# A four-layer graph stack on one core: gate rows transposed on VectorE, layer 3 aggregated in four column tiles, a plan that counts tiling changes

## Chip, core and metric

The kernel runs on one core of a Trainium2 chip. The core has five engines that work side by side, each through its own instructions in order: TensorE (matmul; PE in the profile, its weight loads PEld), VectorE (DVE), ScalarE (ACT), GpSimd (POOL) and SyncE (SP, which here only issues DMAs). The metric is the device time of one launch in microseconds, lower is better. All data is f32 unless said otherwise.

## What is computed

32 graphs of 512 nodes with 256 features share one adjacency matrix with self loops. Each graph passes through four attention layers; after each comes a residual sum and a layer norm. Cut to the layers' cores:

```python
# layer 0: 8 heads of 32, with its own residual, norm and a two-matmul block behind it
scores = einsum('fnhd,fmhd->fhnm', q, k) / sqrt(D);  scores = where(adj > 0, scores, -1e9)
t = einsum('fhnm,fmhd->fnhd', softmax(scores), v);   x = layernorm(x + t) ...
# layer 1: one head, additive scores
h = x @ W;  e = leaky_relu(s1[:, :, None] + s2[:, None, :], 0.2);  e = e + (1 - mask) * -1e9
out = softmax(e) @ h
# layer 2: one head, product scores
e = leaky_relu((x @ W1) @ (x @ W2).T, 0.2);  e = where(adj > 0, e, -1e12)
out = relu(softmax(e) @ (x @ W3))
# layer 3: 4 heads of 64, additive scores
e = e_src[:, :, None, :] + e_dst[:, None, :, :];  e = where(e >= 0, e, 0.2 * e), masked
out = elu(softmax(e) @ q)
```

## The kernel before

The launch runs `fast_path` (L630), which computes everything and a flag; `general_path` follows only if the flag says that values were out of bounds, and does not run with these inputs.

**A plan made in the host program.** `fast_path` does not issue instructions as it goes. Each small group of instructions on one engine is entered in a `Plan` (L459) with its engine, an assumed time in ns, what it reads and writes, and a function that issues it. `place` (L522) then simulates the engines and picks, again and again, the group that can start first; among those of one engine that can start at the same time, the one with the earliest due time. When a group is picked, its buffers are assigned and its instructions issued, so the plan fixes the order of every engine's instructions and nothing else. The assumed times never reach the chip. The due time of a group (L1364) is `PACE` times the graph's number plus an offset that is interpolated from eleven numbers (`TENTHS`; others for the first four and the last five graphs). Up to six graphs (`WAYS`) are under way at once; they share 8 PSUM banks, 8 tiles `p` for attention weights and the other buffers at L677. DMAs in flight are a sixth "engine" in the plan.

**Tilings of TensorE.** Matmuls use the array in four ways, which the plan numbers: 0 the full array (projections, aggregation of layers 1 and 2, transposes); 1 four row tiles of 32 (`exps`, L1027: scores of four heads of layer 0 at once); 2 four column tiles of 32 (aggregation of layer 0, L1093, and the row sums with the constant `pick`, L1065 and L1281); 3 two column tiles of 64 (aggregation of layer 3, L1306). The plan adds `SWITCH` (100 ns) to TensorE's time when the tiling changes. `STAY`, which could put off a change, is 0. An f32 matmul shows as two instructions in the profile.

**Gates of layers 1 and 3** (`gates`, L1167). Their scores are sums of a source and a target term, so the weights are products of exponentials. For the source side the kernel needs exp(0.8 s) of all 512 nodes as a row, on every partition. ScalarE computes it with nodes on partitions into `gs` (L1179, 4 or 16 columns), TensorE transposes `gs` (L1182), ScalarE copies the result from PSUM to `gT` (L1184), SyncE stores `gT` to a DRAM buffer `row` (L1186) in one DMA and loads it back, repeated over all partitions, into `G` (L1192). VectorE then builds the weights from `G` (L1211, L1290) and masks them (L1214, L1297).

**Row sums** of the softmax come for layers 0 and 3 from tiles `p` that DMAs add up (issued by GpSimd, L972) and a few matmuls with `pick`; in the last graph, by matmuls alone. SyncE also issues a copy for them (L1112), the loads of x (L1347) and the stores of the output (L1354).

Of the kernel before, what the change touches and what calls it, by code (L numbers as in the profile page):

```python
# [17 lines left out]
P = 128  # L18
# [12 lines left out]
PACE = 81.87  # L31
STAY = 0.00
START = (0, 10.17, 59.24, 97.18, 85.64)
EARLY = 186.52

TENTHS = (0, 35.72, 65.32, 68.92, 152.58, 202.32, 246.27, 266.73, 356.34, 362.66, 490.49)
FIRST = (
    (0, 35.72, 65.32, 62.35, 138.44, 202.98, 246.27, 266.73, 356.34, 362.66, 490.49),
    (-28.44, 35.72, 73.98, 55.02, 197, 202.32, 246.27, 266.73, 356.34, 362.66, 490.49),
    (-31.13, 30.72, 65.32, 68.92, 152.58, 202.32, 246.27, 266.73, 356.34, 362.66, 490.49),  # L40
    (0, 35.77, 65.37, 68.97, 152.63, 202.32, 246.27, 266.73, 356.34, 362.66, 490.49),)
LAST = (
    (0, 35.72, 65.32, 68.92, 152.58, 202.32, 246.27, 266.73, 354.73, 363.36, 490.49),
    (0, 35.72, 65.32, 68.92, 152.58, 202.32, 246.27, 266.73, 356.34, 362.66, 490.49),
    (0, 35.72, 65.32, 68.92, 152.58, 202.26, 246.21, 266.73, 356.34, 412.91, 557.81),
    (-0.21, 35.51, 65.11, 68.71, 152.37, 202.11, 226.96, 232.14, 316.44, 341.17, 500.04),
    (-6.23, 29.49, 59.09, 8.93, 61.49, 76.67, 155.18, 191.54, 257.43, 316.36, 394.47),)
# [391 lines left out]
SIGNAL = 70  # L439
SWITCH = 100  # L440
# [11 lines left out]
class Op:  # L452
    def __init__(self, engine, ns, run, graph, rank, port, lag, tiling):
        self.engine, self.ns, self.run, self.graph, self.rank = engine, ns, run, graph, rank
        self.port, self.lag, self.tiling = port, lag, tiling
        self.then, self.missing, self.slots, self.ready = [], 0, [], 0.0


class Plan:  # L459
# [19 lines left out]
    def __call__(self, engine, ns, run, reads=(), writes=(), port=False, lag=0, tiling=0):  # L479
        op = Op(engine, ns, run, self.graph, self.rank, port, lag, tiling)  # L480
# [41 lines left out]
    def place(self, urgency, ways, stay=0.0, early=1e12, run=True):  # L522
# [13 lines left out]
        port, port_by, end, tiling = 0.0, None, 0.0, 0  # L536
        self.trace = []
# [21 lines left out]
        while todo:  # L559
            choice = None  # L560
            for e, ops in waiting.items():
                found = []
                for op in ops:
# [8 lines left out]
                    if choice and t > choice[0]:  # L572
                        continue
                    wants = {}
                    for s in op.slots:
                        if s.index is None:
                            wants.setdefault(s.kind, []).append(s)
                    if all(safe(op, kind, new) for kind, new in wants.items()):
                        for kind, new in wants.items():
                            t = max(t, sorted(free[kind])[len(new) - 1][0])  # L580
                        if op.tiling != tiling and e is PE:
                            due += stay
                        found.append((t, due, op))
                if found:
                    best = min(found, key=lambda f: f[:2])
                    if choice is None or best[0] < choice[0]:
                        choice = best
            assert choice, "no instruction can be placed: too few buffers"
            t, _, op = choice
            if op.engine is PE and op.tiling != tiling:  # L590
                t, tiling = max(t, engines[PE] + SWITCH), op.tiling
            waiting[op.engine].remove(op)
# [6 lines left out]
            engines[op.engine] = t + op.ns  # L599
            if op.port:  # L600
                port, port_by = t + op.ns, op.engine
            done = t + op.ns + op.lag + SIGNAL
# [7 lines left out]
            for other in op.then:  # L610
                other.missing -= 1
                other.ready = max(other.ready, done if other.engine != op.engine or op.lag
                                  else t + op.ns)
                if not other.missing:
                    waiting[other.engine].append(other)
# [4 lines left out]
            ended[op.graph] = max(ended.get(op.graph, 0.0), t + op.ns + SIGNAL)  # L620
# [9 lines left out]
def fast_path(  # L630
# [50 lines left out]
        "e1": (6, [P, NC * H3]), "gs": (2, [P, NC * H3]), "ri": (3, [P, NC * H0]),  # L681
        "gT": (2, [NC * H3, P]),
# [27 lines left out]
    nc.vector.memset(far, 0.0)  # L710

# [36 lines left out]
    def prepare():  # L748
# [30 lines left out]
        for c in range(NC):  # L779
            dve(690, lambda c=c: nc.vector.tensor_scalar(  # L780
                T(edges)[:, c, :], T(raws[c // 2])[:, c % 2, :].bitcast(I32), 0.0, None, ALU.is_gt),
                [(raws[c // 2], c)], [(edges, c)])
        for m in range(NC):
# [6 lines left out]
            plan(PE, 440, run, [edges], [bank])  # L790
            dve(690, lambda bank=bank, m=m: nc.vector.tensor_copy(T(edge_t)[:, m, :], T(bank)),
                [bank], [(edge_t, m)])
            dve(400, lambda m=m: nc.vector.tensor_scalar(
# [23 lines left out]
        for c in range(NC):  # L817
            off = Slot("e")
            dve(690, lambda c=c, off=off: nc.vector.tensor_tensor(
                T(off), T(edges)[:, c, :], T(raws[c // 2])[:, c % 2, :].bitcast(I32), ALU.not_equal),  # L820
                [edges, (raws[c // 2], c)], [off])
            dve(690, lambda c=c, off=off: nc.vector.tensor_reduce(
# [65 lines left out]
    def evac(dst, to, src, frm, n, writes):  # L888

        act(170 + n * 0.84, lambda: nc.scalar.activation(to(T(dst)), frm(T(src)), AF.Copy),  # L890
            [src], writes)

    def transposed(src, width=0):

        dst = Slot("t")
        for c0 in range(0, NC, 2):
# [7 lines left out]
            plan(PE, 440, run, [(src, c0), (src, c0 + 1)], [bank])  # L904
# [4 lines left out]
    def project_t(w, col, xT, dst, k):  # L909
# [7 lines left out]
        plan(PE, 1720, run, [w, xT], [bank])  # L917
        evac(dst, lambda t: t[:, k, :], bank, lambda b: b, N, [(dst, k)])

    def project(xT, w, col, width, dst):  # L920

        per = N // width
        for c0 in range(0, NC, per):
# [9 lines left out]
            plan(PE, per * KC * width * 1.69, run, [w, xT], [bank])  # L933
# [4 lines left out]
    def normalise(y, dst):  # L938

        st, mv, rs, nm = Slot("st"), Slot("mv"), Slot("rs"), Slot("rs")  # L940
        for c in range(NC):
# [3 lines left out]
            dve(600, run, [(y, c)], [(st, c), (mv, c)])  # L945
# [3 lines left out]
        act(420, deviations, [mv], [rs])  # L949
        dve(300, lambda: nc.vector.scalar_tensor_tensor(  # L950
            T(nm), T(mv)[:, :, 0], -1.0, T(rs), ALU.mult, ALU.mult), [mv, rs], [nm], True)
        for c in range(NC):
            act(600, lambda c=c: nc.scalar.activation(  # L953
# [3 lines left out]
    def add(dst, a, b, c0, row=None, op=ALU.add):  # L957

        w = slice(c0, c0 + 2)
        pool(1500 if row is None else 1850, lambda: nc.gpsimd.tensor_tensor(  # L960
# [17 lines left out]
    def sums_back(sm):  # L978
# [8 lines left out]
        plan(PE, 440, run, [sT], [bank])  # L987
# [19 lines left out]
    def heads_out(oT, rinv, heads):  # L1007
# [3 lines left out]
        for c0 in range(0, NC, 2):  # L1011
# [7 lines left out]
            plan(PE, 440, run, [oT, rinv], [bank])  # L1019
            dve(680, lambda bank=bank, c0=c0: nc.vector.tensor_tensor(  # L1020
# [6 lines left out]
    def exps(kT, qT, g, m, p):  # L1027
# [8 lines left out]
        plan(PE, 970, run, [(kT, g), (qT, g)], banks, tiling=1)  # L1036
        for j in range(J):
            act(600, lambda j=j: nc.scalar.activation(  # L1038
# [14 lines left out]
    def layer0(xs, at_once):  # L1053
# [14 lines left out]
        def collect(g, m, ps):  # L1068

            if at_once:  # L1070
                for c in (m - 1, m):
                    plan(PE, 870, lambda c=c: sums(g, ps[c], g == 0 and c == 0,
# [8 lines left out]
        for g in range(KC):  # L1081
            av, ps = Slot("bank"), []
            for m in range(NC):
                p = Slot("p")
                exps(kT, qT, g, m, p)
                dve(2420, lambda p=p, m=m: nc.vector.tensor_tensor(  # L1086
# [9 lines left out]
                plan(PE, 880, run, [(v, m), p], [av], tiling=2)  # L1096
# [9 lines left out]
        else:  # L1106
# [7 lines left out]
            plan(PE, 870, lambda: sums(2, low, True, True), [low], [sm], tiling=2)  # L1114
# [3 lines left out]
        dve(370, lambda: within(T(rinv)[:, :NC * H0], R_MIN, R_MAX), [rinv], [], True)  # L1118
# [12 lines left out]
        for d in range(KC):  # L1131
# [6 lines left out]
            plan(PE, 1720, run, [w1_sb, nT], [bank])  # L1138
            act(690, lambda bank=bank, d=d: nc.scalar.activation(
                T(hT)[:, d, :], T(bank), AF.Relu, bias=T(b1_sb)[:, d:d + 1]), [bank, b1_sb], [(hT, d)])  # L1140
        f = Slot("y")
        for c0 in range(0, NC, 2):
# [9 lines left out]
            dve(680, lambda bank=bank, c0=c0: nc.vector.tensor_tensor(  # L1152
# [4 lines left out]
        for c0 in range(0, NC, 2):  # L1157
            w, parts = slice(c0, c0 + 2), (c0, c0 + 1)
            dve(690, lambda w=w: nc.vector.tensor_tensor(
                T(f)[:, w, :], T(f)[:, w, :], T(g2_row).unsqueeze(1).to_broadcast([P, 2, C]),  # L1160
                ALU.mult), [(f, c) for c in parts] + [g2_row], [(f, c) for c in parts], True)
            dve(690, lambda w=w: nc.vector.tensor_tensor(
# [4 lines left out]
    def gates(v, heads, G):  # L1167
# [5 lines left out]
        def check():  # L1173
# [4 lines left out]
        gs, bank, gT, row = Slot("gs"), Slot("bank"), Slot("gT"), Slot("row")  # L1178
# [3 lines left out]
        plan(PE, 150, lambda: nc.tensor.transpose(T(bank)[:R, :P], T(gs)[:, :R], ident),  # L1182
             [gs], [bank])
# [253 lines left out]
```

## Time and profile before

| what | value |
|---|---|
| median of 3 runs | 2895.84 us (2895.43 to 2897.85) |
| profiled execution: span, first to last instruction | 2891.7 us |
| mean granted TensorE clock | 0.993 |
| L1182 gate transposes on TensorE | 64, mean 272 to 276 ns each, pipelined |
| L1184 copies of them on ScalarE | 64, mean 252 to 253 ns |
| L1186 stores of the gate rows | 64 DMAs of 2 or 8 KB, issue 317 ns (median) |
| L1306 aggregation of layer 3 | 1024 instructions, 242.8 us busy |
| L1093 aggregation of layer 0 | 2048 instructions, 275.2 us busy |
| L1034 scores of layer 0 | 2048 instructions, 302.6 us busy |
| wait of VectorE for a gate row, L1211 | 27.6 us in 21 times |

The span is that of one profiled execution. The time outside a launch's span cannot be seen in it; the median of the runs lies 4.1 us above the span. A matmul's mean duration includes the pipeline behind it: the next one starts earlier than it ends, so rates are read from one start to the next. In the groups, the numbers after the bar are busy us, mean ns of one, idle us of the engine before them and what ended it.

### The profile page before, as it was taken

The numbers are of one execution on the slowest core, as the hardware profiler recorded it, in microseconds if no ns is written. First come the engines' busy times: TensorE is split into PE (matmuls) and PEld (weight loads), VectorE is DVE, ScalarE is ACT, GpSimd is POOL, SyncE is SP. The second block draws the span as 40 slices with busy tenths as digits, with TensorE's granted clock in tenths as the row PEclk, the third lists the DMA queues.
The fourth block names the chain that finished last, engine by engine and source line by source line (L and its number), as shares of the span: only waits on it lengthen the run. The fifth ranks groups of instructions, "written<-read, shape, count | busy, mean of one in ns | idle before, by whom it ended". The sixth has DMA issues, their size and how long they took to land.

```text
span 2891.7 us, 39629 instructions
## 1 busy us (share of the span) xinstructions
PE 2832.4 (98%) x14014; PEld 1579.2 (55%) x14014; DVE 2443.2 (84%) x4076; ACT 1885.5 (65%) x4104; POOL 865.9 (30%) x962
## 2 busy tenths in 40 slices
PE   8899999999999999999999999999999999999996
PEld 3355555555555555555555555555555555554562
DVE  5568888888888988888988888988888888888877
ACT  4566667666667666666666666666676666676553
POOL 1233333232333232332232333232333323333312
PEclk9999999999999999999999999999999999999998
DMA  6856777777777777777777777776776777775125
GB/s 168 169 110 142 150 159 164 154 144 160 145 161 153 159 149 158 149 160 157 147 152 150 157 157 155 152 160 144 162 157 150 155 153 146 161 163 115 35 55 132
DMA packets 101149, 424.44 MB, mean 147 GB/s; under 512 B 10256, under 2 KB 46224, under 8 KB 59152
## 3 DMA queue, kind: packets, MB, share of 16 engines
q0 software_dynamic: 49600, 325.08, 57.2%
q1 hardware_dynamic: 51344, 96.75, 11.6%
q8 instruction: 113, 1.85, 0.2%
q14 instruction: 92, 0.75, 0.1%
HBM read 63.38 MB, written 17.10 MB: 28 GB/s over the span
## 4 chain that ended last, share of the span: by engine, by line
PE 92%; DVE 3%; DMA 2%; issue 1%; ACT 1%; POOL 0%; SPq 0%; ACTq 0%; DVEq 0%; POOLq 0%
PE bank L929 15%; PE bank L915 11%; PE bank L1034 9%; PE bank L1093 8%; PE bank L1306 8%; PE bank L1221 7%; PE bank L1244 7%; PE bank L1260 7%; PE bank L902 5%; PE bank L1136 4%; PE bank L1148 4%; PE bank L1017 2%; DMA p<-p 1%; PE bank L1281 1%; PE bank L1065 1%
## 5 line engine op out<-in xcount | busy, mean ns | idle before, releaser
L972 POOL DMA_DIRECT2D p<-p x372 | 322.3, 871 | 1787.8 <-DMA p<-p 568.4
L1086 DVE TENSOR_TENSOR p<-p,edge_t 128x2048 f32<-128x2048 f32 x256 | 618.2, 2424 | 59.7 <-ACT p L1038 59.5
L890 ACT ACTIVATE t<-bank 128x512 f32<-128x512 f32 x640 | 373.5, 596 | 384.2 <-PE bank L915 125.4
L1038 ACT ACTIVATE p<-bank 128x512 f32<-128x512 f32 x1024 | 537.9, 599 | 89.2 <-PE bank L1034 87.6
L943 DVE BATCH_NORM_STATS2 st<-y 128x6 f32<-128x256 f32 x768 | 315.9, 411 | 35.6 <-POOL y L960 26.0
L1290 DVE TENSOR_SCALAR p<-p,e,e 128x512 f32<-128x512 f32 x512 | 331.3, 680 | 1.0 <-DMA p<-row 1.0
L960 POOL TENSOR_TENSOR y<-y,x 128x512 f32<-128x512 f32 x192 | 273.7, 1432 | 158.2 <-ACT y L1265 100.1
L1297 DVE TENSOR_TENSOR p<-p,edge_t 128x2048 f32<-128x2048 f32 x128 | 304.9, 2382 | 2.2
L1034 PE MATMUL bank<-t,t 32*128 32x512 f32 x2048 | 302.6, 644 | 0.0
L953 ACT ACTIVATE x<-y,rs,rs 128x256 f32<-128x256 f32 x512 | 277.6, 596 | 24.6 <-DVE rs L950 24.3
L1093 PE MATMUL bank<-p,v 128*32 128x512 f32 x2048 | 275.2, 609 | 12.5 <-DVE p L1086 9.7
L1306 PE MATMUL bank<-p,v 128*64 128x512 f32 x1024 | 242.8, 605 | 3.6 <-DVE p L1297 3.6
L915 PE MATMUL bank<-t,wqkv 128*128 128x512 f32 x512 | 241.6, 595 | 0.7 <-ACT t L890 0.7
L1221 PE MATMUL bank<-v,p 128*128 128x257 f32 x1024 | 237.8, 381 | 0.7 <-DVE p L1214 0.4
L890 ACT ACTIVATE v<-bank 128x264 f32<-128x264 f32 (+2 forms) x384 | 176.5, 460 | 90.2 <-PE bank L929 88.3
L1260 PE MATMUL bank<-v,p 128*128 128x257 f32 x1024 | 227.4, 380 | 0.0
L1244 PE MATMUL bank<-t,t 128*128 128x512 f32 x512 | 225.1, 592 | 0.0
L1221 PEld LDWEIGHTS bank<-v,p 128*128 128x128 f32 x1024 | 189.5, 190 | 40.3 <-issue 16.3
L1260 PEld LDWEIGHTS bank<-v,p 128*128 128x128 f32 x1024 | 194.2, 190 | 28.6 <-issue 1.3
L1034 PEld LDWEIGHTS bank<-t,t 32*128 32x128 f32 x2048 | 86.0, 184 | 169.5 <-issue 101.5
L944 DVE BATCH_NORM_AGGREGATE mv<-st 128x2 f32<-128x6 f32 x768 | 139.7, 182 | 26.3
L902 PE MATMUL bank<-ident,x 128*128 128x128 f32 x1024 | 148.9, 279 | 11.7 <-DMA x<-in_x_dram 7.7
(121 smaller groups left out, 4148.8 us busy)
## 6 DMA issues: line engine op xcount, KB each, us to landing
p<-p POOLq DMA_DIRECT2D x248, 1024.0 KB, 7.2
p<-p POOLq DMA_DIRECT2D x124, 512.0 KB, 5.7
p<-row SPq DMA_DIRECT2D x32, 1024.0 KB
x<-in_x_dram SPq DMA_DIRECT2D x32, 512.0 KB
out_dram<-x SPq DMA_DIRECT2D x32, 512.0 KB
p<-p SPq DMA_DIRECT2D x31, 512.0 KB
e<-row SPq DMA_DIRECT2D x32, 256.0 KB
t<-in_adj_dram SPq DMA_DIRECT2D x4, 256.0 KB
```

The source lines that it names most:

```text
L890: act(170 + n * 0.84, lambda: nc.scalar.activation(to(T(dst)), frm(T(src)), AF.Copy), [src], writes)
L915: nc.tensor.matmul(T(bank), T(w)[:, i, col:col + P], T(xT)[:, i, :], start=(i == 0), stop=(i == KC - 1))
L929: nc.tensor.matmul(T(bank)[:, j * width:(j + 1) * width], T(xT)[:, k, (c0 + j) * P:(c0 + j + 1) * P], T(w)[:, k, col:col + width], start=( ...
L1034: nc.tensor.matmul(T(banks[j]), T(kT)[r, g, m * P:(m + 1) * P], T(qT)[r, g, :], start=True, stop=True)
L1038: act(600, lambda j=j: nc.scalar.activation(T(p)[:, j, :], T(banks[j]), AF.Exp, scale=1.0 / math.sqrt(D0)), [banks[j]], [(p, j)])
L1086: dve(2420, lambda p=p, m=m: nc.vector.tensor_tensor(T(p), T(p), T(edge_t)[:, m, :].unsqueeze(1).to_broadcast([P, J, N]), ALU.mult), [p, ( ...
L1093: nc.tensor.matmul(T(av)[j * D0:(j + 1) * D0, :], T(v)[:, m, h * D0:(h + 1) * D0], T(p)[:, j, :], start=(m == 0), stop=(m == NC - 1))
L1221: nc.tensor.matmul(T(bank)[:, :C + 1], T(p)[:, m, c * P:(c + 1) * P], T(v)[:, m, 2:C + 3], start=(m == 0), stop=(m == NC - 1))
L1244: nc.tensor.matmul(T(bank), T(xT)[:, k, m * P:(m + 1) * P], T(qT)[:, k, :], start=(k == 0), stop=(k == KC - 1))
L1260: nc.tensor.matmul(T(bank)[:, :C + 1], T(p)[:, m, c * P:(c + 1) * P], T(v)[:, m, :C + 1], start=(m == 0), stop=(m == NC - 1))
L1290: nc.vector.tensor_scalar(T(p)[:, 2 * m + i, :], T(G)[:, h, :], T(e1)[:, r:r + 1], T(e02)[:, r:r + 1], ALU.mult, ALU.max)
L1306: nc.tensor.matmul(T(av)[i * D3:(i + 1) * D3, :], T(q)[:, m0 + m, 2 * H3 + h * D3:2 * H3 + (h + 1) * D3], T(p)[:, 2 * m + i, :], start=(m0 ...
```

## The change

1. `gates`: the transpose of `gs` on TensorE and ScalarE's copy are replaced by one transpose on VectorE, which turns 32x32 blocks. `gs` and `gT` become 128x32 tiles; `gs` is cleared once at the start by GpSimd. Since each block of 32 nodes ends up on its own 32 partitions, the store becomes four DMAs, with 32 values to a row.
2. Layer 3's aggregation uses four column tiles of 32 (tiling 2) in place of two of 64 (tiling 3). Twice as many matmuls of half the width compute the same thing.
3. The plan's order. When it picks a group for TensorE, the key is now the due time, plus an entry from `CHANGE` by the tilings left and entered, plus `LATE` times the wait of TensorE, in which a change counts at least `SWITCH` plus an entry time. Due times have an offset for each of a graph's 339 groups (`DUE`), with additions for the first four and last five graphs. The assumed times of nearly all groups are new numbers, each group has an additional `tail` until others see its result, and `START`, `PACE` and `EARLY` are new.

The row sums are computed as before. Of part 3 the diff shows the rules and some of the many new assumed times:

```diff
-PACE = 81.87
-STAY = 0.00
-START = (0, 10.17, 59.24, 97.18, 85.64)
-EARLY = 186.52
-TENTHS = (0, 35.72, 65.32, 68.92, 152.58, 202.32, 246.27, 266.73, 356.34, 362.66, 490.49)
+PACE = 82.89
+EARLY = 237.58
+LATE = 58.47
+CHANGE = ((0, -15.02, -0.86), (-10.53, 0, -9.19), (16.15, -1.96, 0))
+START = (13.01, 7.41, 43.1, 109.34, 103.14)
+DUE = (
...
-SIGNAL = 70
-SWITCH = 100
+SIGNAL = 40
+SWITCH = 92
+ENTRY = {1: 121, 2: 34}
+TAIL = {PE: 160, DVE: 85, ACT: 120, POOL: 45, SP: 0, DMA: 0}
...
-    def __call__(self, engine, ns, run, reads=(), writes=(), port=False, lag=0, tiling=0):
-        op = Op(engine, ns, run, self.graph, self.rank, port, lag, tiling)
+    def __call__(self, engine, ns, run, reads=(), writes=(), port=False, lag=0, tiling=0, entry=104):
+        op = Op(engine, ns, run, self.graph, self.rank, port, lag, tiling, ENTRY.get(tiling, entry))
...
-                    if choice and t > choice[0]:
+                    if e is not PE and choice and t > choice[0]:
                         continue
...
+                    key = t, due
+                    if e is PE:
+                        wait = t - engines[PE]
+                        if op.tiling != tiling:
+                            wait = max(wait, SWITCH) + op.entry
+                        key = due + change[tiling][op.tiling] + late * wait, 0
+                    if best and key >= best[0]:
+                        continue
                     if all(safe(op, kind, new) for kind, new in wants.items()):
-                        for kind, new in wants.items():
-                            t = max(t, sorted(free[kind])[len(new) - 1][0])
-                        if op.tiling != tiling and e is PE:
-                            due += stay
-                        found.append((t, due, op))
...
-            done = t + op.ns + op.lag + SIGNAL
+            done = t + ns + op.lag + op.tail + SIGNAL
...
-        "e1": (6, [P, NC * H3]), "gs": (2, [P, NC * H3]), "ri": (3, [P, NC * H0]),
-        "gT": (2, [NC * H3, P]),
+        "e1": (6, [P, NC * H3]), "gs": (2, [P, 32]), "ri": (3, [P, NC * H0]),
+        "gT": (2, [P, 32]),
...
+    for gs in buffers["gs"]:
+        nc.gpsimd.memset(gs, 0.0)
...
-        plan(PE, 970, run, [(kT, g), (qT, g)], banks, tiling=1)
+        plan(PE, 858, run, [(kT, g), (qT, g)], banks, tiling=1)
         for j in range(J):
-            act(600, lambda j=j: nc.scalar.activation(
+            act(482, lambda j=j: nc.scalar.activation(
...
-        gs, bank, gT, row = Slot("gs"), Slot("bank"), Slot("gT"), Slot("row")
+        gs, gT, row = Slot("gs"), Slot("gT"), Slot("row")
...
-        plan(PE, 150, lambda: nc.tensor.transpose(T(bank)[:R, :P], T(gs)[:, :R], ident),
-             [gs], [bank])
-        act(270, lambda: nc.scalar.activation(T(gT)[:R, :], T(bank)[:R, :P], AF.Copy),
-            [bank], [gT])
-        plan(SP, 450, lambda: nc.sync.dma_start(T(row)[:R, :], T(gT)[:R, :]), [gT], [row], lag=2000)
+        dve(70, lambda: nc.vector.transpose(T(gT), T(gs)), [gs], [gT])
+
+        def store():
+            with nc.allow_non_contiguous_dma(reason="32 values a row"):
+                for j in range(0, P, 32):
+                    nc.sync.dma_start(T(row)[:R, j:j + 32], T(gT)[j:j + R, :])
+        plan(SP, 600, store, [gT], [row], lag=2000)
...
-                            h = 2 * k + i
-                            nc.tensor.matmul(T(av)[i * D3:(i + 1) * D3, :],
-                                             T(q)[:, m0 + m, 2 * H3 + h * D3:2 * H3 + (h + 1) * D3],
-                                             T(p)[:, 2 * m + i, :], start=(m0 + m == 0),
-                                             stop=(m0 + m == NC - 1))
-                plan(PE, 1770, run, [q, p], [av], tiling=3)
+                            for w in range(i * D3, (i + 1) * D3, 32):
+                                nc.tensor.matmul(T(av)[w:w + 32, :],
+                                                 T(q)[:, m0 + m, 2 * H3 + k * P + w:2 * H3 + k * P + w + 32],
+                                                 T(p)[:, 2 * m + i, :], start=(m0 + m == 0),
+                                                 stop=(m0 + m == NC - 1))
+                plan(PE, 1742, run, [q, p], [av], tiling=2)
...
     def due(b, rank):
-        times = FIRST[b] if b < len(FIRST) else LAST[b - B] if b >= B - len(LAST) else TENTHS
-        tenth = min(int(when[rank]), 9)
-        return PACE * b + times[tenth] + (times[tenth + 1] - times[tenth]) * (when[rank] - tenth)
+        late = FIRST[b] if b < len(FIRST) else LAST[b - B] if b >= B - len(LAST) else None
+        time = PACE * b + DUE[rank]
+        if late:
+            tenth = min(int(when[rank]), 9)
+            time += late[tenth] + (late[tenth + 1] - late[tenth]) * (when[rank] - tenth)
+        return time
...
-        plan.place(urgency, WAYS, 1e3 * STAY, 1e3 * EARLY)
+        plan.place(urgency, WAYS, 1e3 * EARLY, LATE, [[1e3 * c for c in row] for row in CHANGE])
```

## The prediction

> **What bounds it now.** I read the page first, for its busy shares, its clock row and its chain.
>
> ```profile
> span 2891.7 us, 39629 instructions
> ...
> PE 2832.4 (98%) x14014; PEld 1579.2 (55%) x14014; DVE 2443.2 (84%) x4076; ACT 1885.5 (65%) x4104; POOL 865.9 (30%) x962
> ...
> PEclk9999999999999999999999999999999999999998
> ...
> PE 92%; DVE 3%; DMA 2%; issue 1%; ACT 1%; POOL 0%; SPq 0%; ACTq 0%; DVEq 0%; POOLq 0%
> ```
>
> TensorE is busy for 98% of the span and makes up 92% of the chain that ended last. Next come the waits of TensorE, longest first, and the busy times between 200 and 2600 us.
>
> ```profile
> PE bank L1093 <- DVE p L1086: 9.7, 6, 2.7
> PE bank L902 <- DMA x<-in_x_dram: 7.7, 1, 7.7
> PE bank L1306 <- DVE p L1297: 3.6, 2, 2.3
> ```
> ```profile
> 200.00:2600.00 2400.00, 2396.53 (x11954) 1346.36 (x11951) 2093.00 (x3425) 1609.93 (x3518) 742.30 (x826) 1.00 0.72 153
> ```
>
> TensorE idles 3.5 us in these 2400 at a full clock, so there the kernel is a queue of matmuls, and only taking matmul time away can shorten it. All idle time of TensorE is 2891.7 - 2832.4 = 59.3 us, nearly all in the first 200 and the last 190 us. But a busy TensorE isn't one that streams. The chain gives the bare rate, and the timeline of TensorE what is lost between groups (start us, length, engine, line, names, shape, count).
>
> ```profile
> 191.46 6.87 PE bank L1244 x16
> ```
> ```profile
> 1503.54 3.65 PE L1306 MATMUL bank<-p,v 128*64 128x512 f32 x16
> 1507.13 1.07 PE L1065 MATMUL bank<-p,pick 128*32 128x512 f32 x8
> 1508.12 1.14 PE L1034 MATMUL bank<-t,t 32*128 32x512 f32 x8
> 1509.19 0.65 PE L985 MATMUL bank<-ident,e 128*128 128x128 f32 x4
> 1509.69 0.60 PE L902 MATMUL bank<-ident,x 128*128 128x128 f32 x4
> 1510.12 1.04 PE L929 MATMUL bank<-l1w,t 128*128 128x258 f32 x4
> 1511.00 1.03 PE L1017 MATMUL bank<-ident,t 128*128 128x128 f32 x8
> 1511.96 1.94 PE L1306 MATMUL bank<-p,v 128*64 128x512 f32 x8
> ```
>
> Sixteen matmul instructions in 6.87 us are 429 ns for each 512-column stream. Read the timeline from start to start: L1306 in pairs is 8 streams, 3.43 us, and takes 3.59; L1065 in fours is 2 streams, 0.86, and takes 0.99; L1034 in fours 0.86, and takes 1.07; L985 to L902, both 128*128, comes at 0.50 against 4 x 109 = 0.44, and L902 to L929 at 0.43, with nothing lost. So time goes where the shape of the tiles changes. I took all PE rows from 200 to 2600 us in order of start, cut them into visits (runs of one tiling; the small gate transposes count as full-array work) and subtracted the streams. A visit's loss, entry and exit together, and visits per graph (a graph takes 87.05 us there, so 27.57 graphs): row tiles (L1034) 213 ns, 8.0; four column tiles 138 ns, 9.0; two column tiles (L1306) 152 ns, 3.0; full array 157 ns for transposes to 200 ns for matmuls, 178 taken as the mean, 12.2. That is 32.2 visits and about 6.0 us of 87.05; the streams are 81.1. Over the whole span: streams 2617, 32 x 6.0 = 192, idle 59; what is left, some 23 us, is about the 0.7% that the mean granted clock of 0.993 takes.
>
> **Part by part.** Gate transposes: L1182 has 64 instructions, one stream of 109 ns each, so 32 x 2 x 0.109 = 7.0 us leave TensorE. In 26 of 27 graphs layer 3's gate stands between row tiles and four column tiles, and its visit costs a further 98 ns, 3 us in all. ScalarE loses the copy L1184 (252 ns x 64 = 16 us), which is off the path. VectorE gets 64 transposes of 128x32. No row shows one; the reciprocal of 128x32 (L994, 357 ns) and the 128x4 multiply (L950, 233 ns) bound it, and I take 0.3 us, or 0.6 us a graph. VectorE idles 2400 - 2093 = 307 us there, 11.1 us a graph, which hides it. Without that cover it would cost 64 x 0.3 = 19 us. The transpose waits for ScalarE's gs at the head of VectorE's queue, with the mask products of other graphs behind it; before, TensorE's queue held that wait (2.2 us median from L1179 to L1182).
>
> Store: four DMAs instead of one, 192 more issues of 0.317 us on SyncE, so the gate row's load L1192, and behind it the loads of x, the outputs and the copy L1112, come at least 0.95 us later. SyncE now waits 1.42 us (median) from the store to L1192. If the four land together, G is 0.95 us late; if one after the other, 4 x 1.42 - 1.42 + 0.95 = 5.2 us. I take 1 us, as they are independent. Of SyncE's time 2371 us are waits at L1112 and L1186, so the issues are free. Who waits next is VectorE, at L1211 and L1290 (28.6 us so far), within its slack. The two memsets of gs on GpSimd (0.1 to 0.4 us each by L1207 and L1237) lie under the 7.7 us wait for the first x.
> The pieces shrink from 512 to 128 bytes. The Trainium skill (DMA: Bandwidth & Descriptors, Specifications) says that transfers under 512 bytes make the DMA engine read, modify and write; no row here shows its price, and the sum would not change, since G's lateness is hidden in the sum.
>
> Layer 3 in four column tiles: 16 instructions in fours are 4 streams of 429 ns, as 8 in pairs are now. Where four column tiles follow a group of the same tiling (L1281 to L1093) the next stream starts after 429 ns, so I take no loss; bounds are 0 and the 24 ns that the first stream of such a visit has extra (453). The visit is 14 ns cheaper than before (138 against 152), and the 1.9 junctions a graph from L1306 to four column tiles vanish.
> Against this part speaks the Trainium skill (TensorE: Matmul & The Clock Gate, Part 3): three column tiles of 32 by 512 gave 2.38 times the rate, not 3. By that a stream of four would take 429 x 3/2.38 = 541 ns, which over 16 streams a graph is 1.8 us, 57 us in all, and the time would be about 2884 us. The trace disagrees (429), and I go by it.
>
> The plan: only order changes. In the new key a change from tiling a to b costs CHANGE plus 58.47 times the switch (92 ns plus entry). Full to row -15.02 + 12.45 = -2.6 us of due time; full to column +6.5; row to full +0.9; row to column -1.8; column to row +10.5; column to full +27.6. So TensorE is held in four column tiles as long as any such group can start within 27.6 us of due time, where the old key counted nothing (STAY is 0). A graph has 14 such groups now (8 of layer 0, 4 of layer 3, 2 of sums) against 12.0 visits; with the junctions gone 10.1. I take 7.2, halving their number against 14, since masks arrive 2.4 us apart (L1086) and p tiles run out when held. Each visit saved takes a full-array visit with it: 12.2 - 1.0 (gate) - 2.9 = 8.3. Row tiles take 4 of 8 banks, which ScalarE must empty at 0.6 us each, so they hardly merge: 7.6. In all 23.1 visits: 7.6 x 213 + 7.2 x 138 + 8.3 x 178 ns = 4.09 us against 6.0, a gain of 1.91, plus 0.22 of streams, 2.13 us a graph.
>
> Start and end: new START, FIRST and LAST move what stands in the first 200 us (idle 25.0 us) and the last 190 (29.8). No row prices an order; bounds are those 55 us either way; I take nothing, and 15 us for the range.
>
> **Sum.** 2891.7 - 32 x 2.13 = 2823.5; the median lies 4.1 us above the profiled span; together 2827.7, say 2828 us.
>
> **Rivals.** *Structure alone:* buffers and dependences leave nothing to merge. Then 1.9 junctions (124 ns each), the gate and the cheaper visits give 0.36 + 0.22 = 0.58 us a graph, 18.6 us: 2877. For it: p tiles limit what can wait. Against: the 27.6 us. *Deep merging:* 6 row, 5 column, 6 full visits cost 3.04 us, a gain of 2.96 + 0.22, 102 us: 2794. For it: TensorE has six graphs to choose from; against: the banks. *Slower, through the gate row:* G comes late at the head of VectorE's in-order queue, twice a graph. VectorE's slack at the new pace is 11.1 - 2.1 = 9.0 us a graph, so TensorE starves once each gate is over 4.5 us late, and the kernel is slower from about 5.7 us on, where 2.3 us a graph eat the gain. At 6.5 us: 13 - 9 = 4 us a graph, 128 - 68 = +60: 2956. For it: the upper bound of 5.2 us is close; against: independent stores. *Swapped for waits:* TensorE holds for a group that the chip brings later than the plan thinks, and idles what it saves, 68 us: 2896. Against: today's plan, with cruder times, loses 3.5 us in 2400.
>
> **Chances.** Forecast (2805 to 2855) 0.60, structure alone 0.14, deep 0.12, swapped 0.05, slower 0.09. What this measurement can tell from no change is about 0.2%, 5.8 us: faster 0.86, same 0.04, slower 0.10. The range leaves out most of the slow cases and the deepest merging: 2795 to 2872, with structure's 2877 and the edges' 15 us at its borders.
>
> **What would show it.** A period between graphs near 84.9 us instead of 87.05; no TensorE row for the gates; L1306's successor with 32 columns at 429 ns a stream of four; some 23 visits a graph, the full-array and column ones fewer, the row ones as many. Wrong, if streams of four take longer than 429 ns, if TensorE's waits grow past 60 us, if VectorE waits for G for over 4.5 us a gate, or if the visits stay near 29.

## The result, and the profile after

The changed kernel takes 3021.99 us (median of 4 runs, 3019.23 to 3025.08) against 2895.64 us before: a ratio of 1.0431, 95% interval 1.0416 to 1.0446. It is slower by 126 us, outside the predicted range and on the other side. The page of the changed kernel, with the lines that answer to those of before:

```profile
span 3017.2 us, 42035 instructions
...
PE 2856.9 (95%) x14974; PEld 1597.7 (53%) x14974; DVE 2441.6 (81%) x4140; ACT 1838.4 (61%) x4040; POOL 988.2 (33%) x964
...
PE 58%; DVE 28%; issue 5%; DMA 5%; ACT 3%; POOL 1%; SPq 0%; DVEq 0%; ACTq 0%; POOLq 0%
PE bank L973 10%; DVE p L1336 10%; PE bank L1306 7%; PE bank L1267 7%; PE bank L1078 7%; PE bank L959 6%; DVE p L1343 5%; DVE p L1130 5%; PE bank L1137 5%; PE bank L1290 4%; PE bank L946 3%; PE bank L1352 3%; PE bank L1192 2%; DVE st L987 2%; DMA p<-p 2%
```

TensorE was 92% of the chain that ended last and is now 58%; VectorE went from 3% to 28%. VectorE's busy time is the same to 2 us (2443.2 before), but not its parts: the weights of layer 3 (L1336) take 417.3 us where they took 331.3, and the masks of layers 0 and 3 (L1130, L1343) 884.6 where they took 923.1. The weights and their mask (L1343) head its share of the chain. Between 200 and 2600 us this shows as idle time of TensorE (first the busy us of each engine, clock, DMA share; then TensorE's longest waits in that stretch, with their total, number and longest):

```profile
200.00:2600.00 2400.00, 2325.01 (x12223) 1303.73 (x12221) 2005.37 (x3346) 1504.10 (x3323) 828.11 (x792) 0.99 0.70 147
```
```profile
PE bank L1352 <- DVE p L1343: 48.5, 16, 4.3
PE bank L1137 <- DVE p L1130: 14.8, 29, 4.1
```

TensorE idles 75.0 us there, 3.5 before. Its clock, granted in full there before, drops to 0.5 in 16 pieces of 3.4 or 6.8 us, 64.8 us in all, half of which, 32 us, is lost; over the whole span the mean clock fell from 0.993 to 0.981. To see where the 125.5 us of span went, I took the start of layer 2's aggregation (L1260 before, L1306 after) of graphs 5 and 26 as marks. Up to graph 5 the changed kernel needs 660.3 us instead of 618.6 (+41.7), the 21 graphs after it 90.78 us each instead of 87.28 (+73.5), and the rest 450.5 instead of 440.3 (+10.3).

One graph's worth of the loss, on VectorE, GpSimd and TensorE (start us, length, engine, line, operation):

```profile
1185.21 8.12 DVE L1336 TENSOR_SCALAR p<-p,e,e 128x512 f32<-128x512 f32 x4
1193.37 2.29 DVE L1343 TENSOR_TENSOR p<-p,edge_t 128x2048 f32<-128x2048 f32 x1
```
```profile
1185.23 1.95 POOL L1016 DMA_DIRECT2D p<-p  x2 [6.26 <-PE bank L1180]
1186.42 2.06 POOL L1004 TENSOR_TENSOR y<-y,g_row 128x512 f32<-128x512 f32 x1
1187.95 1.34 POOL L1016 DMA_DIRECT2D p<-p  x1
1188.57 3.26 POOL L1004 TENSOR_TENSOR y<-y,bb_row 128x512 f32<-128x512 f32 x2
1191.12 1.92 POOL L1004 TENSOR_TENSOR x<-x,be_row 128x512 f32<-128x512 f32 x1
```
```profile
1190.09 1.90 PE L1352 MATMUL bank<-p,v 128*32 128x512 f32 x16
1195.71 2.79 PE L1352 MATMUL bank<-p,v 128*32 128x512 f32 x12 [3.73 <-DVE p L1343]
```

Four L1336, which take 0.54 us each at the median, take 8.12 us together: the first two 0.53 and 0.54, the last two, beside GpSimd's tensor operations, 2.66 and 4.63. The mask follows at 1193.37, and TensorE, which finished its last layer 3 group, stands still for 3.73 us until it is done. This one meeting repeats: 12 times in the stretch TensorE waits 3.7 to 4.3 us at L1352, each time behind a pair of L1336 of 2.6 to 2.7 and 4.6 to 4.7 us, 45 of the 75.0 us. In the kernel before no wait in the stretch is over 1 us. The drops of the clock go with it: 14 of the 16 lie at a wait of 3.7 us or more, these 12 among them.

The spread of L1336 in the changed kernel is 500/540/4649 ns (least, median, most), its mean 859 ns against 680 before. Sorted by what GpSimd does meanwhile: 377 of the 512 have no tensor operation of GpSimd beside them and take 0.54 us in the mean, at most 0.67, whether it issues DMAs then or not; the other 135 take 1.76 us. Before, 83 had one beside them, and took 1.45 us.

```profile
L1336 DVE TENSOR_SCALAR p<-p,e,e 128x512 f32<-128x512 f32 x512 | 417.3, 859 | 15.3 <-DMA p<-row 15.3
```

The plan behind the order explains why these operations meet. It treats VectorE's two-input and fast operations and GpSimd's tensor operations as users of one port, and never lets two overlap. The Trainium skill says the same of the chip (GPSIMD Engine Reference, Specifications: the SBUF interfaces are shared with VectorE, in contention with two-port or two-input instructions), and the stretched L1336 agree. But the plan fixes only the order within each engine. I compared each group's planned start, which the host program can print, with its start in the trace. The four tensor operations of 1186.42 to 1191.12 us were planned behind the mask; on the chip nothing makes GpSimd wait for it. VectorE ran 65 us behind its plan there, these operations only 62, and so they pushed in between. Such early starts are not new: 245 of GpSimd's 448 groups on the port start before the VectorE group planned ahead of them has ended, and 249 in the kernel before. What differs is what they meet, and what waits for it.

The same comparison gives two more facts. First, the plan by itself never promised a gain: its own end is 2871.2 us, and that of the plan before 2864.4. Each by its own assumed times, both take 86.2 us a graph between the marks, and the new plan puts the first mark 14.3 us later (624.2 against 609.9). Second, the assumed times of VectorE's groups add up to 2493 us in the plan before and 2253 in the new one; the chip's VectorE is busy for 2443 and 2442. For GpSimd they add up to 1071 and 865, and it is busy for 866 and 988. So the old plan's sums had room for the collisions and the new one's have none. That this room is what kept the old order safe fits, but no run changes the assumed times alone. At its end the old order ran 30 us behind its plan, the new one 150.

### The profile page after: what moved, and what is told of

Same layout as the page of the kernel before. It is cut to its first block, busy times and chain, and to the rows that moved or that the text cites. A ratio compares the mean times of both kernels' runs of the same rounds, so it can differ in the third digit from the quotient of the medians.

```text
span 3017.2 us, 42035 instructions
## 1 busy us (share of the span) xinstructions
PE 2856.9 (95%) x14974; PEld 1597.7 (53%) x14974; DVE 2441.6 (81%) x4140; ACT 1838.4 (61%) x4040; POOL 988.2 (33%) x964
## 4 chain that ended last, share of the span: by engine, by line
PE 58%; DVE 28%; issue 5%; DMA 5%; ACT 3%; POOL 1%; SPq 0%; DVEq 0%; ACTq 0%; POOLq 0%
PE bank L973 10%; DVE p L1336 10%; PE bank L1306 7%; PE bank L1267 7%; PE bank L1078 7%; PE bank L959 6%; DVE p L1343 5%; DVE p L1130 5%; PE bank L1137 5%; PE bank L1290 4%; PE bank L946 3%; PE bank L1352 3%; PE bank L1192 2%; DVE st L987 2%; DMA p<-p 2%
## 5 line engine op out<-in xcount | busy, mean ns | idle before, releaser
L1016 POOL DMA_DIRECT2D p<-p x372 | 334.8, 955 | 1203.2 <-DMA p<-p 314.3
L1130 DVE TENSOR_TENSOR p<-p,edge_t 128x2048 f32<-128x2048 f32 x256 | 589.6, 2305 | 122.5 <-ACT p L1082 121.3
L1004 POOL TENSOR_TENSOR y<-y,x 128x512 f32<-128x512 f32 x192 | 320.4, 1678 | 464.2 <-DVE y L1064 231.3
L1336 DVE TENSOR_SCALAR p<-p,e,e 128x512 f32<-128x512 f32 x512 | 417.3, 859 | 15.3 <-DMA p<-row 15.3
L1078 PE MATMUL bank<-t,t 32*128 32x512 f32 x2048 | 317.7, 650 | 2.2 <-DVE e L1295 1.6
L1352 PE MATMUL bank<-p,v 128*32 128x512 f32 x2048 | 263.4, 636 | 50.1 <-DVE p L1343 49.4
L1343 DVE TENSOR_TENSOR p<-p,edge_t 128x2048 f32<-128x2048 f32 x128 | 295.0, 2305 | 4.1
L1137 PE MATMUL bank<-p,v 128*32 128x512 f32 x2048 | 268.3, 606 | 27.7 <-DVE p L1130 27.6
L1290 PE MATMUL bank<-t,t 128*128 128x512 f32 x512 | 245.6, 608 | 0.0
L1306 PE MATMUL bank<-v,p 128*128 128x257 f32 x1024 | 229.1, 380 | 1.7 <-ACT p L1299 1.7
L934 ACT ACTIVATE v<-bank 128x258 f32<-128x258 f32 (+2 forms) x384 | 173.4, 455 | 78.0 <-PE bank L973 77.6
L1306 PEld LDWEIGHTS bank<-v,p 128*128 128x128 f32 x1024 | 193.7, 190 | 40.3 <-issue 14.0
L1299 ACT ACTIVATE p<-e,shift 128x512 f32<-128x512 f32 x128 | 91.9, 720 | 184.8 <-DVE e L1297 184.7
L1352 PEld LDWEIGHTS bank<-p,v 128*32 128x32 f32 x2048 | 60.9, 114 | 198.2 <-issue 114.7
```

Of the source, the lines that this page charges most:

```text
L934: act(55 + n * 0.83, lambda: nc.scalar.activation(to(T(dst)), frm(T(src)), AF.Copy), [src], writes)
L1078: nc.tensor.matmul(T(banks[j]), T(kT)[r, g, m * P:(m + 1) * P], T(qT)[r, g, :], start=True, stop=True)
L1130: dve(2205, lambda p=p, m=m: nc.vector.tensor_tensor(T(p), T(p), T(edge_t)[:, m, :].unsqueeze(1).to_broadcast([P, J, N]), ALU.mult), [p, ( ...
L1137: nc.tensor.matmul(T(av)[j * D0:(j + 1) * D0, :], T(v)[:, m, h * D0:(h + 1) * D0], T(p)[:, j, :], start=(m == 0), stop=(m == NC - 1))
L1306: nc.tensor.matmul(T(bank)[:, :C + 1], T(p)[:, m, c * P:(c + 1) * P], T(v)[:, m, :C + 1], start=(m == 0), stop=(m == NC - 1))
L1336: nc.vector.tensor_scalar(T(p)[:, 2 * m + i, :], T(G)[:, h, :], T(e1)[:, r:r + 1], T(e02)[:, r:r + 1], ALU.mult, ALU.max)
```

## The experiments

Two theories stood against each other. *Port theory*: GpSimd's tensor operations, earlier than planned, hold VectorE's weights back, and TensorE waits. *Order theory*: the new order brings the weights too late in any case. A third, that the new instructions themselves cost the time, was tested apart, in the order of before. The order of a kernel can't be mixed from parts of both plans: with the new key left out, or assumed times a few per cent longer, the plan's own end became 4 to 6 ms. So all kernels below keep one of the two orders exactly, and change instructions or add waits in it. The ratios are to runs of before made beside each kernel (medians 2896.3 to 2897.8 us).

| kernel | order | median us | ratio to before (95%) | us a graph, 5 to 26 |
|---|---|---|---|---|
| before | before | 2895.64 | | 87.28 |
| changed | new | 3021.99 | 1.0431 (1.0416 to 1.0446) | 90.78 |
| after_thin | new | 2923.42 | 1.0094 (1.0077 to 1.0111) | 86.59 |
| after_port | new | 2950.53 | 1.0179 (1.0162 to 1.0196) | 87.82 |
| after_two | new | 3043.99 | 1.0496 (1.0465 to 1.0528) | 91.42 |
| before_thin | before | 2886.60 | 0.9962 (0.9948 to 0.9976) | 86.84 |
| both_k | before | 2968.87 | 1.0255 (1.0238 to 1.0272) | 89.35 |
| tiles_k | before | 2894.93 | 0.9992 (0.9982 to 1.0002) | 86.97 |
| gate_k2 | before | 2893.64 | 0.9985 (0.9975 to 0.9994) | 87.02 |
| store4 | before | 2903.74 | 1.0017 (1.0006 to 1.0028) | 87.22 |
| both_k2 | before | 2889.34 | 0.9971 (0.9958 to 0.9983) | 86.93 |
| both_port | before | 2869.50 | 0.9905 (0.9883 to 0.9926) | 86.24 |

**after_thin and before_thin: most of GpSimd's adding taken away.** Both leave out most of the residual, bias and shift terms (the cut is shown shortened):

```diff
-            T(dst)[:, w, :], T(a)[:, w, :],
-            T(b)[:, w, :] if row is None else ...
+            T(dst)[:, w, :n], T(a)[:, w, :n],     # n = 16 where dst is a, else 256
+            T(b)[:, w, :n] if row is None else ...
```

> The changed kernel in its own order, but GpSimd's in-place adds (10 of its 12 tensor operations a graph) work on 16 of 256 columns, so most of the residual, bias and shift terms are left out. Port theory (GpSimd's tensor operations start earlier on the chip than the plan has them, hold VectorE's weights L1336 back, and these are late for TensorE): L1336 falls from a mean of 859 ns to under 600, TensorE's waits for VectorE in L1343 and L1130 fall from 77 us to under 25, and the time to 2860 to 2920 us. Order theory (the new order brings the weights too late even without collisions): above 2980 us, with the waits still there.

> The control: the same thin adds in the kernel before, in its own order. Port theory: its order has room for the collisions, so TensorE's idle time hardly moves, 2885 to 2897 us. Order theory: the same. A gain like that of the changed kernel would mean that thin adds are a gain anywhere and say nothing of the change.

The changed kernel wins 99 us with thin adds, the kernel before 9 us against its 2895.64. The time is 3 us above the range that the port theory gave, and 57 below the order theory's bound. L1336 (L1337 here) is down to a mean of 664 ns, not under 600: 90 of the 512 still have a tensor operation of GpSimd beside them, the other 422 take 0.54 us, beside DMA issues too. TensorE's waits at the two aggregations, L1352 and L1137 in the changed kernel, fall from 77 us to 18, under the 25 expected. The second heads the list (L1138 here); behind it stands one wait for layer 3's mask, in the row sums of the last graph (L1328; 8.0 us in the changed kernel):

```profile
PE bank L1138 <- DVE p L1131: 16.1, 18, 2.7
PE bank L1328 <- DVE p L1344: 13.2, 1, 13.2
```

From 500 to 2500 us VectorE falls only 9 us further behind its plan here (28 to 37); in the changed kernel it falls 111 (23 to 134). So in the stretch where all graphs overlap, nearly the whole loss goes when GpSimd's adds get short. This run can't tell the collisions from the adds' own length; after_port can.

What the pair also shows: thinned, the changed kernel takes 86.59 us a graph, and the kernel before 86.84. These 0.25 us are order and instructions together. In the order of before, the two new instructions alone take 0.35 us off a graph (both_k2 below: 87.28 to 86.93). So no run shows a gain of the new order by itself.

**after_port: the collisions ordered instead of removed.** Shortened:

```diff
             if run and op.run:
+                if op.port and op.engine is POOL and self.last:
+                    nc.gpsimd.tensor_copy(seen, <first value that self.last wrote>)
+                    self.last = None
                 op.run()
+                if op.port and op.engine is DVE and op.writes:
+                    self.last = op
```

> The changed kernel in its own order, but each GpSimd tensor group that the plan puts behind a VectorE group of the shared port first copies one value of that group's result, so it can't start earlier than planned. Port theory: L1336 falls below 650 ns in the mean, and the time to 2880 to 2960 us. Order theory: 3020 us or more, since more instructions and waits are added.

The computation is complete here, and 71 of the 126 us are back, although 296 small copies were added. L1336 (L1353 here) takes 646 ns in the mean and at most 1.46 us, and GpSimd's adds are hardly stretched: the in-place add falls from a mean of 1678 to 1306 ns.

```profile
L1004 POOL TENSOR_TENSOR y<-y,x 128x512 f32<-128x512 f32 x192 | 320.4, 1678 | 464.2 <-DVE y L1064 231.3
```
```profile
L1021 POOL TENSOR_TENSOR y<-y,x 128x512 f32<-128x512 f32 x192 | 249.6, 1306 | 85.8 <-ACT y L1328 50.1 <-DVE y L1081 18.0 <-ACT y L1398 17.6
L1353 DVE TENSOR_SCALAR p<-p,e,e 128x512 f32<-128x512 f32 x512 | 308.2, 646 | 36.6 <-DMA p<-row 32.0 <-DMA p<-p 4.1 <-PE bank L1307 0.4
```

The first line is the changed kernel's, the other two after_port's. The order theory's 3020 us or more is excluded. From 500 to 2500 us this kernel falls 35 us further behind its plan, with all the adds in place, against 111 and after_thin's 9. So ordering the collisions brings back two thirds of that loss; what makes up the rest, the held GpSimd or the meetings that remain, was not separated.

**both_k: the instructions alone, first try.** The order of before, with the VectorE transpose issued where the plan has ScalarE's copy, four stores, four column tiles. Of the cut:

```diff
-        plan(PE, 150, lambda: nc.tensor.transpose(T(bank)[:R, :P], T(gs)[:, :R], ident), ...
-        act(270, lambda: nc.scalar.activation(T(gT)[:R, :], T(bank)[:R, :P], AF.Copy), ...
+        plan(PE, 150, lambda: None, ...
+        act(270, lambda: nc.vector.transpose(T(gT), T(gs)), ...
```

> The kernel before with its own order of groups, in which only the instructions are changed: gates transposed on VectorE with four stores, layer 3 in four column tiles. If the loss came from the slower gate row or the narrower tiles, this kernel has it: 2920 us or more. Port and order theory, by which both parts are harmless: 7 us of gate streams, 3 us of their visits and about 7 us of junctions from two to four column tiles are gained, 2875 to 2886 us.

This took 71 us more than before, which looked as if the instructions were to blame. The waits of VectorE say what happened, before above and both_k below:

```profile
DVE p L1211 <- DMA e<-row: 27.6, 21, 7.0
```
```profile
DVE p L1216 <- DMA e<-row: 135.2, 28, 10.3
```

The transpose stood too far back in VectorE's queue: in layer 1 it started 6.0 us after `gs` was ready (ScalarE's copy, in its place before, after 3.8), and the load of G was issued 10.0 us after `gs` instead of 5.3; in layer 3, 11.0 instead of 6.3. The gate row was late, by my placing of it. In the changed kernel the transpose starts 0.3 us after `gs` and the load is issued after 2.8 us, earlier than before, so this is not its loss. The run shows something else: 4.7 us of lateness at each of the two gates cost 2.1 us a graph, although VectorE idles 11 us a graph.

**tiles_k, gate_k2, store4, both_k2: the parts apart.** `tiles_k` has only the four column tiles. `gate_k2` has only the gates, with the transpose right behind `gs`:

```diff
-        act(220, lambda: nc.scalar.activation(T(gs)..., AF.Exp, scale=0.8), scores, [gs])
+        def turned():
+            nc.scalar.activation(T(gs)..., AF.Exp, scale=0.8)
+            nc.vector.transpose(T(gT), T(gs))
+        act(220, turned, scores, [gs, gT])
```

`store4` keeps the transposes on TensorE and cuts the store:

```diff
-        plan(SP, 450, lambda: nc.sync.dma_start(T(row)[:R, :], T(gT)[:R, :]), ...
+                for j in range(0, P, 32):
+                    nc.sync.dma_start(T(row)[:R, j:j + 32], T(gT)[:R, j:j + 32])
```

> The kernel before in its own order, with four column tiles in layer 3 as its only edit. If the tiles are harmless, the junctions from L1306 to column tiles vanish and the time is 2886 to 2892 us, with no new wait of TensorE. If streams of four are slower than pairs (541 against 429 ns), 2940 us or more.

> The kernel before in its own order, with gates on VectorE and four stores as its only edit; the transpose stands in VectorE's queue directly behind ScalarE's gs, not 4 us later as in both_k. If both_k lost its 71 us because its transposes stood too late, the gate row is now as early as before or earlier and the time is 2880 to 2896 us. If four small stores or a transpose in VectorE's queue make the row late by themselves, above 2910 us, with VectorE waiting over 60 us for the gate row of layer 1.

> The kernel before, its transposes on TensorE, with the store of a gate row cut into four DMAs as its only edit. It prices the store alone: three further issues of 0.32 us and the landing of four pieces. If only the issues count, the row comes 1 us later, VectorE's wait for it grows from 28 to about 50 us, and the time stays within 2893 to 2905 us. If the pieces land much later, 2910 us or more.

> The kernel before in its own order with both edits, the transpose directly behind gs. If both parts are harmless where the gate row is in time: the sum of the two gains, 2872 to 2888 us, the fastest of all. If the store of four pieces makes the row late in this order: above 2905 us.

`tiles_k` can't be told from before (2894.93 us, above the 2886 to 2892 expected, the interval reaching past 1); its visits to column tiles lose 138 ns at the median when their streams of four are taken at 429 ns, as before, so these run at that rate. `gate_k2` is faster by 0.15%, `store4` slower by 0.17% (the smaller store's price, 6 us, with 52.4 us of VectorE's waits for the row of layer 1 instead of 27.6), and `both_k2` faster by 0.29%, 1 us above its range. So neither new instruction carries the loss in the order of before.

**after_two: the tiles undone in the new order.** Two column tiles of 64 in place of four in L1352, order as in the changed kernel.

> The changed kernel in its own order, with layer 3 back in two column tiles of 64 as its only edit. If four column tiles cost nothing, as tiles_k says, TensorE gets some more changes of tiling and the time is 3015 to 3040 us. If they are part of the loss, under 3005 us.

It is 22 us slower than the changed kernel, 4 us more than the range allows: so the four tiles don't carry the loss in the new order either; undoing them costs time.

**both_port: the fastest.** `both_k2` with GpSimd held behind VectorE as in after_port.

> both_k2 (order of before, both edits) with GpSimd's tensor groups held behind VectorE's as in after_port. If the order of before has room for the collisions, holding GpSimd wins little or nothing: 2880 to 2895 us. If collisions cost it as they cost the changed order, 2870 us or less. Above 2900 us if the held GpSimd becomes late itself.

It beats both kernels: 2869.50 us, 0.95% under before and just inside the branch in which collisions cost the old order too. L1314, the weights of layer 3, now takes 547 ns in the mean and never over 1259, where both_k2 has up to 2422. TensorE idles 0.6 us in the 2400:

```profile
200.00:2600.00 2400.00, 2399.37 (x12875) 1350.03 (x12874) 1986.70 (x3525) 1617.99 (x3496) 765.56 (x1079) 1.00 0.73 155
```
```profile
L1314 DVE TENSOR_SCALAR p<-p,e,e 128x512 f32<-128x512 f32 x512 | 262.4, 547 | 6.2 <-DMA p<-row 6.2
```

The gain over both_k2, 20 us, is larger than the idle time it had left in that stretch (2400 - 2393.0 = 7.0 us). Beyond its streams TensorE spent 170 us there in both_k2, idle time included, and 152 in both_port, at almost the same number of visits (816 and 818). The difference sits in visits that lose over 0.4 us: 48 in both_k2, 2 in both_port. I read them as waits too short to show between the modelled ends of matmuls. Why the copies win more here than thin adds did in before_thin (9 us) was not looked into.

## Why the prediction was wrong

**What bounds it** was right for the kernel before. **Gate transposes and tiles** were right in kind: the TensorE rows are gone, the VectorE transpose takes 203 ns (0.3 us assumed, and below the bounds of 0.233 and 0.357), streams of four take 429 ns and a visit of column tiles costs 138 ns. The 2.38 times for three tiles of the Trainium skill (TensorE: Matmul & The Clock Gate, Part 3) does not carry over to this stream; going by the trace was right. **The store** was priced within its bounds: its four issues span 1.0 to 1.3 us at the median, and VectorE's waits for the row are 25.7 us in the changed kernel.

**The step that failed is "The plan: only order changes".** It priced the new order by visits alone. The visits were mis-sized: 700 in 2400 us at 90.78 us a graph are 26.5 a graph, not 23.1; by the prices per visit of the prediction (8.0 row, 8.3 column, 10.2 full) they cost 4.7 us instead of 4.09. The gain was also taken from the wrong side: 6.0 us was today's measured loss, while the prediction's own prices make today's visits 5.6, because 178 ns for a full-array visit is too little (208 at the median). Like for like, 1.5 us a graph were forecast and not 1.9, and 0.9 came. What made it wrong by sign is what the step left at nothing: that another order brings other waits. Against the gain of 1.1 us a graph with the streams stand 4.6 us of waits and lower clock (90.78 - 87.28 + 1.1). Of these, 2.7 are TensorE's idle time (75.0 us against 3.5 in the stretch) and 1.2 the half clock that goes with it (32 us); the rest was not taken apart. The prediction's own sign of being wrong, waits over 60 us, came true in that stretch alone.

The rival *swapped for waits* had the mechanism in general and 5% of the chance, dismissed with the words that today's plan, "with cruder times, loses 3.5 us in 2400". That says nothing of the new times. The cruder times were longer than the chip's in sum, 2493 us for VectorE against 2443 measured, and I take that surplus to have kept the order safe, though no run isolates it. The new times are closer to an undisturbed instruction and 190 us short of what VectorE takes with GpSimd beside it. The profile of before had the sign of it, the weights of layer 3 at 680 ns in the mean:

```profile
L1290 DVE TENSOR_SCALAR p<-p,e,e 128x512 f32<-128x512 f32 x512 | 331.3, 680 | 1.0 <-DMA p<-row 1.0
```

Undisturbed, one takes 0.54 us, and the next starts 0.45 us after it. The new plan assumes these 457 ns, the old one 560, both less than the 647 that each took of VectorE's busy time. I looked at that diff as better measured.

The rival *through the gate row* was wrong for this kernel, where the row comes earlier than before, but both_k shows that its mechanism sets in earlier than I let it: I had VectorE's idle time cover what is late. By that, 4.7 us at each gate, 9.4 a graph, would have cost nothing at the pace of before, with its 11.1 us of idle time; it cost 2.1 us a graph, 71 us in all. Idle time in an in-order queue isn't cover for one instruction that is late.

**Start and end**, taken as nothing with 15 us for the range, cost +41.7 and +10.3 us. Of the start, 14.3 us stand in the new plan itself. after_thin still needs 653.2 us to graph 5, and after_port 652.7, so collisions are only 7 or 8 of the 41.7. In after_thin VectorE falls 28 us behind the plan in the first 500 us (6 in the kernel before). It does so in steps: 12 us of its idle time there are waits for the gate rows of graphs 0, 2 and 4 (8 us for all rows in the kernel before), and others fall on weights loaded at the start and row sums added by DMA. No run took these apart; the cause of the rest of the slower start stays open, as does the share of the new due times against the new key.

## What to carry to other kernels

A static order holds only what the chip also enforces: where a plan keeps two engines off one port by time alone, add a real dependence, however small. Such copies won 71 us in the new order and some 20 us in the old one. Assumed times that are longer than an undisturbed instruction can be slack, not error: before making them exact, compare the engine's planned total with its busy time in the trace. Print the plan's own end and pace before forecasting a gain from it. And price a reordering by the waits that it can make as well as by the work that it saves; idle time of an in-order engine is no proof of slack.

## What the runs showed of the hardware

A VectorE operation (tensor_scalar, 128x512 f32) of 0.54 us took up to 4.65 us beside GpSimd's tensor operations, which themselves grew from 1.27 to as much as 3.44 us: both sides stretched. Beside GpSimd's DMA issues alone it took at most 0.67 us. Around TensorE's waits of 3.7 to 4.3 us in the changed kernel the granted clock was 0.5 for 3.4 or 6.8 us (0.50 from 1195.5 to 1198.9 us, at the wait shown above), so such a wait costs more than its length. The transpose of 128x32 on VectorE took 203 ns. A visit of TensorE to another tiling cost 138 ns (four column tiles) and 213 ns (row tiles) at the median in both orders.
